# Graph attention with residual and normalisation: late residuals on VectorE, two normalisations on GpSimd, and the last block's leading column searched in halves

## The chip, the cores and the metric

The kernel runs on one core of a Trainium2 chip. The metric is the time of one execution on the device in microseconds; lower is better. The times before are the median of three runs; the profile is of one further execution with the hardware profiler on.

## The reference

```python
def reference(x, adj, W, a):            # x 4096x512, adj 4096x4096, W 512x2048, a 4x1024x1, all float32
    ht  = (x @ W).reshape(N, 4, 512).transpose(1, 0, 2)
    src = einsum('hnd,hd->hn', ht, a[:, :512, 0]); dst = einsum('hnd,hd->hn', ht, a[:, 512:, 0])
    e   = leaky_relu(src[:, :, None] + dst[:, None, :], 0.01) + adj[None]
    g   = einsum('hij,hjd->hid', softmax(e), ht).mean(axis=0)
    x   = x + g
    return (x - mean(x)) / sqrt(var(x) + 1e-5)          # over the 512 columns of each row
```

`adj` is zero or uniform up to 1e9, with a filled diagonal, and is added to the scores ahead of the softmax. Where the largest entry of a row of `adj` leads the second largest by more than the scores can make up for, the softmax is one at that entry's column and zero elsewhere. The row's result is then `layernorm(x[i] + x[column] @ mean over heads of W)`.

## The kernel before, in words

Rows are split into 32 blocks of 128 (`NB`), one row of each block per partition. `leading_rows` treats every row as one with a leading entry and tests that on the side; a second function, `general`, computes the full softmax for blocks in which the test failed, behind a branch that these inputs don't take.

The schedule is written out by hand: engines execute their instructions in the order of the program text. For each step `t` of a loop over the 32 blocks:

- SP's queue issues the load of block `t + 5` of `adj` (2 MB; the last block in four pieces of 128x1024).
- VectorE takes the maxima of segments of 32 columns (`segment_maxima`, L163), then the top 8 of the 128 maxima and their positions (`find_segment`, L170 and L172). GpSimd works out the segment's row in memory (L174) and fetches the segment (`lead`, L176), and works out where it starts (L181).
- Two steps later VectorE takes the fetched segment's top 8 (`inner`, L192; for the blocks from 24 on this is done after the loop) and searches the leading value in it (`find_column`, L198); GpSimd adds the two positions (L200) and gathers the rows of `x` at the leading columns (`y`, L186).
- Three steps later TensorE turns those rows (`turn`, L213), ScalarE copies them out of PSUM (`yt`, L215), and TensorE multiplies them by the mean of `W` over the heads (`products`, L228). The residual is added on TensorE, as a product of the identity with the rows of `x` (`residual`, L221), into the same PSUM tile.
- ScalarE takes mean and variance (`stats`, L250 and L252), GpSimd the factors (`rstd`, L255 to L257), ScalarE normalises (`finish`, L261), and the result goes out from `hold`.

In the code `BEHIND` is 24 and `LATE` is 28. Blocks 24 to 27 have their products put by in SBUF (`put_by`), and the residual is added from there after the loop, on GpSimd for 24 to 26 and on VectorE for 27 (`add_x`, L244). Blocks 28 to 31 are finished after the loop, with VectorE's own statistics (`moments`, L281 and L285) and normalisation (`factor` and `normalise`, L290 and L297). Block 28 and block 29 get their residual on TensorE in the last step of the loop; block 30 on VectorE (L511); block 31 on TensorE, in two halves of 256 columns (`residual_in_halves`, L266).

For block 31 the column isn't searched in the fetched segment but in the whole row, while its segment is fetched for the second largest value only:

```python
    def find_column_in_row(ib):
        col = small.tile([P, 8], U32, name="col")
        nc.vector.max_index(col, top[:, ib, :], adj_t[ib])
        gather_rows(ib, col)
```

The test that all rows have a leading entry needs a bound from the norms of the rows of `x` (`row_norm`, L235). The functions `bound`, `test`, `count` and `report` (L367 to L401) go back and forth between VectorE, TensorE and ScalarE in the midst of the last blocks. The stores of the last blocks are issued by SP in a fixed order: block 28, block 29, blocks 24 and 25, block 30, blocks 26 and 27, block 31.

Of the kernel before, what the change touches and what calls it, by code (L numbers as in the profile page):

```python
# [9 lines left out]
F32 = mybir.dt.float32  # L10
U32 = mybir.dt.uint32
# [9 lines left out]
P = 128  # L21
# [45 lines left out]
def leading_rows(ctx, tc, x, adj, W, a, out, ident, v, n_bad, any_bad):  # L67
# [36 lines left out]
    w_sum = once.tile([P, KB, D], F32, name="w_sum")  # L104
    a_rows = once.tile([2 * H, D], F32, name="a_rows")

    once.tile([P, 32], F32, name="pad_end")
    adj_t = {}

    def pieces(ib):  # L110
# [36 lines left out]

    top = once.tile([P, NB, 8], F32, name="top")
    inner = once.tile([P, NB, 8], F32, name="inner")
    xx = once.tile([P, NB], F32, name="xx")  # L150
    nm = once.tile([P, NB], F32, name="nm")
    sd = once.tile([P, NB], F32, name="sd")
# [4 lines left out]
    def segment_maxima(ib, lo, hi):  # L157

        if lo == 0:
            seg_of[ib] = small.tile([P, S], F32, name="seg")  # L160
        n = max(pieces(ib), 2)
        for k in range(lo * n // PIECES, hi * n // PIECES):
            nc.vector.tensor_reduce(  # L163
                seg_of[ib][:, ts(k, S // n)],
                adj_t[ib][:, ts(k, N // n)].rearrange("p (s e) -> p s e", e=E), axis=AX.X, op=OP.max,
            )

    def find_segment(ib):
        seg = seg_of.pop(ib)
        nc.vector.max(out=top[:, ib, :], in_=seg)  # L170
        at = small.tile([P, 8], U32, name="at")
        nc.vector.max_index(at, top[:, ib, :], seg)  # L172
        row = small.tile([P, 1], U32, name="row")
        nc.gpsimd.tensor_tensor(row, at[:, 0:1], first[:, ib : ib + 1], op=OP.add)  # L174
        lead = lead_pool.tile([P, E], F32, name="lead")
        nc.gpsimd.indirect_dma_start(  # L176
            out=lead, out_offset=None, in_=adj_segs,
            in_offset=bass.IndirectOffsetOnAxis(ap=row[:, :1], axis=0),
        )
        start = at_of[ib] = small.tile([P, 1], U32, name="start")  # L180
        nc.gpsimd.tensor_tensor(start, at[:, 0:1], width, op=OP.mult)  # L181
        lead_of[ib] = lead

    def gather_rows(ib, col):
        y = y_t[ib] = y_pool.tile([P, D], F32, name="y")
        nc.gpsimd.indirect_dma_start(  # L186
            out=y, out_offset=None, in_=x,
            in_offset=bass.IndirectOffsetOnAxis(ap=col[:, :1], axis=0),
        )
# [10 lines left out]
        nc.gpsimd.tensor_tensor(col, at_of.pop(ib), within[:, 0:1], op=OP.add)  # L200
        gather_rows(ib, col)

    def find_column_in_row(ib):

        col = small.tile([P, 8], U32, name="col")
        nc.vector.max_index(col, top[:, ib, :], adj_t[ib])
        gather_rows(ib, col)

    def turn(ib):
        y = y_t.pop(ib)  # L210
        tp = psum.tile([P, KB, P], F32, name="tp", bufs=2)
        for kb in range(KB):
            nc.tensor.transpose(tp[:, kb, :], y[:, ts(kb, P)], ident)  # L213
        yt = yt_of[ib] = rows.tile([P, KB, P], F32, name="yt")
        nc.scalar.copy(yt, tp)  # L215

    def residual(ib):
        start = ib not in o_ps
        if start:
            o_ps[ib] = psum.tile([P, D], F32, name="o")  # L220
        nc.tensor.matmul(o_ps[ib], ident, hold[:, ib, :], start=start, stop=False)  # L221

    def products(ib, lo=0, hi=KB):
        start = ib not in o_ps
        if start:
            o_ps[ib] = psum.tile([P, D], F32, name="o")
        for kb in range(lo, hi):
            nc.tensor.matmul(  # L228
                o_ps[ib], yt_of[ib][:, kb, :], w_sum[:, kb, :],
                start=(start and kb == 0), stop=(kb == KB - 1),  # L230
            )
# [11 lines left out]
    def add_x(engine, ib):  # L243
        engine.tensor_add(hold[:, ib, :], hold[:, ib, :], o_ps["by"][:, ib - BEHIND, :])  # L244
        o_ps[ib] = hold[:, ib, :]
# [8 lines left out]
    def rstd(i):  # L254
        nc.gpsimd.tensor_scalar(sd[:, i], sd[:, i], 1.0 / D, EPS, op0=OP.mult, op1=OP.add)  # L255
        nc.gpsimd.tensor_tensor(sd[:, i], sd[:, i], power[:, : i.stop - i.start], op=OP.pow)  # L256
        nc.gpsimd.tensor_mul(nm[:, i], nm[:, i], sd[:, i])  # L257

    def finish(ib):
        i = slice(ib, ib + 1)  # L260
        nc.scalar.activation(hold[:, ib, :], o_ps.pop(ib), AF.Identity, bias=nm[:, i], scale=sd[:, i])  # L261

    def residual_in_halves(ib):
        o_ps[ib] = [psum.tile([P, D // 2], F32, name="o") for _ in range(2)]
        for k, o in enumerate(o_ps[ib]):
            nc.tensor.matmul(o, ident, hold[:, ib, ts(k, D // 2)], start=True, stop=False)  # L266
# [10 lines left out]
    def moments(ib):  # L277

        if ib < NB - 1:
            st = small.tile([P, nc.vector.BN_STATS_DIM], F32, name="st", bufs=2)  # L280
            nc.vector.bn_stats(st, o_ps[ib])  # L281
        else:
            st = halves_st
        mv = mean_var[ib] = small.tile([P, nc.vector.BN_AGGR_DIM], F32, name="mv", bufs=3)
        nc.vector.bn_aggr(mv, st)  # L285
        r = rt[ib] = sd[:, ib : ib + 1]
        nc.scalar.activation(r, mv[:, 1:2], AF.Sqrt, bias=eps)

    def factor(ib, shift=False):
        nc.vector.reciprocal(rt[ib], rt[ib])  # L290
        if shift:
            nc.vector.scalar_tensor_tensor(
                nm[:, ib : ib + 1], mean_var[ib][:, 0:1], -1.0, rt[ib], op0=OP.mult, op1=OP.mult
            )

    def normalise(ib, o, columns=slice(0, D)):
        nc.vector.tensor_scalar(  # L297
            hold[:, ib, columns], o, mean_var[ib][:, 0:1], rt[ib], op0=OP.subtract, op1=OP.mult
        )
# [108 lines left out]
    for t in range(NB):  # L408
        if t == NB // 2:
            tc.mark_branch_hint_location("general", engines=HINTED)  # L410
        if t in x_at:
            load_x(*x_at[t])
        if t + AHEAD == NB - 1:
            load_x(LATE, Q)
        load_adj(t + AHEAD)
        middle = 1 if t == NB - 1 else 2
        segment_maxima(t, 0, middle)
        if t >= COLUMN:
            find_column(t - COLUMN)
        segment_maxima(t, middle, PIECES)  # L420
        pair = FINISH <= t < BEHIND + FINISH and t % 2 == 0
        if pair:
            rstd(slice(t - FINISH, t - FINISH + 2))
        if t == NB - 1:
            for ib in (BEHIND, BEHIND + 2):
                load_x(ib, 2)
        find_segment(t)
        if t < 2:
            mean_of_heads(t)
        elif t == 2:  # L430
            mean_of_heads(2)
            mean_of_heads(3)
        if t == 0:
            turn_a()
        turned = [(*vectors[0], turn_w(*vectors.pop(0))) for _ in range(vectors_at.get(t, 0))]
        if t == 16:
            head_norms()
        ib = t - PROJECT
        if t == NB - 1:
            for late in range(LATE, NB):  # L440
                row_norm(late)
            residual(LATE)
            residual(LATE + 1)
        if ib >= 0:
            turn(ib)
            if ib > BEHIND:
                products(ib - 1, KB - 1, KB)
            if ib < BEHIND:
                residual(ib)
        for some in turned:  # L450
            head_vector(*some)
        if ib >= 0:
            products(ib, 0, KB if ib < BEHIND else KB - 1)
        if t >= BEHIND + STATS:
            put_by(t - STATS)
        elif t >= STATS:
            stats(t - STATS)
            row_norm(t - STATS)
        if pair:
            finish(t - FINISH)  # L460
            finish(t - FINISH + 1)
# [6 lines left out]
        store(nc.sync, ib, 2)  # L468
    find_column(NB - 2)
    add_x(nc.gpsimd, BEHIND)  # L470
    add_x(nc.gpsimd, BEHIND + 1)
    find_column_in_row(NB - 1)
    add_x(nc.gpsimd, BEHIND + 2)
    products(LATE, KB - 1, KB)
    residual_in_halves(NB - 1)
    turn(NB - 3)
    products(NB - 3, 0, KB - 1)
    moments(LATE)
    for ib in range(BEHIND, NB):
        find_inner(ib)  # L480
    bound(0)
    products(NB - 3, KB - 1, KB)
    stats(BEHIND)
    factor(LATE)
    normalise(LATE, o_ps.pop(LATE))
    bound(1)
    turn(NB - 2)
    bound(2)
    add_x(nc.vector, LATE - 1)
    stats(BEHIND + 1)  # L490
    moments(LATE - 1)
    products(NB - 2, 0, 2)
# [4 lines left out]
    stats(BEHIND + 2)  # L497
    rstd(slice(BEHIND, BEHIND + 2))
    rstd(slice(BEHIND + 2, BEHIND + 3))
    moments(NB - 3)  # L500
    report(pg)
    turn(NB - 1)
# [5 lines left out]
    products(NB - 2, KB - 1, KB)  # L508
    products_of_half(NB - 1, 0)
    products_of_half(NB - 1, 1)  # L510
    nc.vector.tensor_add(hold[:, NB - 2, :], o_ps[NB - 2], hold[:, NB - 2, :])  # L511
    o_ps[NB - 2] = hold[:, NB - 2, :]
    moments(NB - 2)
    stats_of_half(NB - 1, 0)
    factor(NB - 2)
    normalise(NB - 2, o_ps.pop(NB - 2))
    finish(BEHIND + 2)
    finish(BEHIND + 3)
    stats_of_half(NB - 1, 1)
    moments(NB - 1)  # L520
    factor(NB - 1, shift=True)
# [157 lines left out]
```

## Time and profile before

| What | Value |
|---|---|
| median of 3 runs | 236.11 us (235.84 to 236.12) |
| profiled execution | 236.21 us, of which span 234.6 us |
| TensorE (PE) busy | 195.2 us, 83% |
| VectorE (DVE) busy | 188.4 us, 80% |
| ScalarE (ACT) busy | 111.6 us, 48% |
| GpSimd (POOL) busy | 101.2 us, 43% |
| DMA | 97.21 MB, 414 GB/s over the span |
| granted TensorE clock, mean | 0.975 |

Busy shares are means over the whole span. The DMA engines are busy nine tenths or more from the second slice of 40 to the last but two, and the page's chain of work that ended last is DMA for 45% of the span. The timeline lists instructions with start and duration in microseconds from the span's start; a bracket gives the engine's idle time just before and what ended it. L-numbers are lines of the kernel before.

### The profile page before, as it was taken

Reading aid. Unit: us, or ns where it says so; the run is one execution under the profiler, and the core shown is the slowest. Engines: PE = TensorE matmul, PEld = TensorE weight load, DVE = VectorE, ACT = ScalarE, POOL = GpSimd, SP = SyncE. Lnnn points to the kernel's source line nnn. Section 1 sums busy time; section 2 is a strip of 40 time slices with the busy share of each in tenths; the row PEclk is TensorE's granted clock in tenths of the full one; section 3 lists DMA queues with packets and bytes.
Section 4 is the critical chain, followed back from the end, with each engine's and each line's share of the span. In section 5 each row is a group of like instructions: output and inputs, shape, how many; then the busy total and the mean of one; then the engine's idle time right before and its main releaser. Section 6 shows DMA issues by size and latency. Waiting matters only on the chain.

```text
span 234.6 us, 2498 instructions
## 1 busy us (share of the span) xinstructions
PE 195.2 (83%) x683; PEld 101.4 (43%) x683; DVE 188.4 (80%) x302; ACT 111.6 (48%) x267; POOL 101.2 (43%) x215
## 2 busy tenths in 40 slices
PE   0188929999999999999979879797998968698990
PEld 0034514756565655555534333242443423244460
DVE  1736875589869995999589989998799999989672
ACT  2012011255474747474758354646464645166582
POOL 1012232414527462646353645464365464549130
PEclk9999977999999999999999999999799999999998
DMA  6999999999999999999999999999999999999985
GB/s 226 439 428 426 443 425 430 415 440 412 440 420 426 424 437 434 425 424 428 427 432 433 425 433 422 432 418 429 425 432 418 422 425 427 411 425 419 417 355 210
DMA packets 13697, 97.21 MB, mean 414 GB/s; under 512 B 2152, under 2 KB 2664, under 8 KB 7792
## 3 DMA queue, kind: packets, MB, share of 16 engines
q1 hardware_dynamic: 10080, 88.08, 88.9%
q0 software_dynamic: 3584, 8.92, 9.6%
q8 instruction: 6, 0.10, 0.2%
q14 instruction: 11, 0.09, 0.1%
q10 hardware_dynamic: 16, 0.02, 0.0%
HBM read 88.62 MB, written 8.39 MB: 414 GB/s over the span
## 4 chain that ended last, share of the span: by engine, by line
DMA 45%; POOL 17%; issue 15%; PE 10%; DVE 9%; ACT 1%; POOLq 0%; SPq 0%; DVEq 0%
DMA adj_t<-in_adj_dram 42%; DVE seg L163 8%; PE o L228 7%; POOL lead L176 6%; POOL y L186 5%; DMA y<-in_x_dram,col 3%; POOL sd L256 2%; PE o L270 2%; POOL start L181 1%; POOL row L174 1%; POOL col L200 1%; PE tp L213 1%; PE o L221 1%; ACT yt L215 1%; POOL sd L255 1%
## 5 line engine op out<-in xcount | busy, mean ns | idle before, releaser
L163 DVE TENSOR_REDUCE seg<-adj_t 128x64 f32<-128x2048 f32 (+1 forms) x68 | 146.0, 2149 | 32.7 <-DMA adj_t<-in_adj_dram 32.3
L228 PE MATMUL o<-w_sum,yt 128*128 128x512 f32 x248 | 115.1, 605 | 1.7 <-ACT yt L215 1.7
L228 PEld LDWEIGHTS o<-w_sum,yt 128*128 128x128 f32 x248 | 44.5, 191 | 54.8 <-issue 42.3
L215 ACT COPY yt<-tp 128x512 f32<-128x512 f32 x32 | 18.8, 588 | 44.3 <-PE tp L213 44.3
L176 POOL DMA_INDIRECT lead<-in_adj_dram,row x32 | 32.3, 1010 | 15.5 <-POOL row L174 15.0
L186 POOL DMA_INDIRECT y<-in_x_dram,col x32 | 30.9, 965 | 15.4 <-POOL col L200 15.2
L318 PE MATMUL o<-hold,ident 128*128 128x512 f32 x32 | 18.9, 745 | 17.5 <-DMA hold<-in_L_gnn_W_dram 17.5
L213 PE MATMUL tp<-ident,y 128*128 128x128 f32 x128 | 20.0, 280 | 12.6 <-DMA y<-in_x_dram,col 12.6
L221 PE MATMUL o<-hold,ident 128*128 128x512 f32 x52 | 27.3, 611 | 0.0
L213 PEld LDWEIGHTS tp<-ident,y 128*128 128x128 f32 x128 | 14.9, 143 | 25.4 <-issue 25.0
L174 POOL TENSOR_TENSOR row<-at,first 128x1 uint32<-128x1 uint32 x32 | 6.1, 190 | 42.0 <-DVE at L172 42.0
L336 ACT COPY wt<-tp 128x512 f32<-128x512 f32 x16 | 9.2, 587 | 31.4 <-PE tp L334 31.4
L200 POOL TENSOR_TENSOR col<-start,within 128x1 uint32<-128x1 uint32 x31 | 5.9, 190 | 40.1 <-DVE within L198 40.1
L235 ACT ACTIVATE sq<-hold 128x512 f32<-128x512 f32 x32 | 19.8, 619 | 0.0
L342 PEld LDWEIGHTS pv<-at_d,wt 128*128 128x128 f32 x128 | 16.3, 191 | 6.8 <-ACT wt L336 4.0
L318 PEld LDWEIGHTS o<-hold,ident 128*128 128x128 f32 x32 | 7.4, 243 | 26.7 <-POOL row L174 11.0
L319 ACT ACTIVATE w_sum<-o 128x512 f32<-128x512 f32 x4 | 2.4, 598 | 33.9 <-PE o L318 33.9
L261 ACT ACTIVATE hold<-o,nm,sd 128x512 f32<-128x512 f32 x24 | 17.2, 771 | 0.0
L252 ACT ACTIVATE sq<-o,nm 128x512 f32<-128x512 f32 x24 | 16.5, 688 | 0.8
L342 PE MATMUL pv<-at_d,wt 128*128 128x2 f32 x128 | 15.3, 244 | 0.6 <-ACT wt L336 0.6
L250 ACT ACTIVATE sq<-o 128x512 f32<-128x512 f32 x24 | 14.6, 609 | 0.0
L334 PEld LDWEIGHTS tp<-ident,hold 128*128 128x128 f32 x64 | 7.9, 142 | 6.9 <-issue 6.9
(85 smaller groups left out, 139.8 us busy)
## 6 DMA issues: line engine op xcount, KB each, us to landing
adj_t<-in_adj_dram SPq DMA_DIRECT2D x27, 2048.0 KB, 31.3
hold<-in_x_dram SPq DMA_DIRECT2D x7, 1024.0 KB, 33.2
adj_t<-in_adj_dram SPq DMA_DIRECT2D x6, 1024.0 KB, 25.7
out_dram<-hold SPq DMA_DIRECT2D x10, 512.0 KB, 15.2
adj_t<-in_adj_dram SPq DMA_DIRECT2D x8, 512.0 KB
hold<-in_L_gnn_W_dram SPq DMA_DIRECT2D x4, 1024.0 KB
out_dram<-hold SPq DMA_DIRECT2D x2, 1024.0 KB
hold<-in_x_dram SPq DMA_DIRECT2D x2, 512.0 KB, 14.1
```

The lines of the kernel that those rows point to most:

```text
L163: nc.vector.tensor_reduce(seg_of[ib][:, ts(k, S // n)], adj_t[ib][:, ts(k, N // n)].rearrange("p (s e) -> p s e", e=E), axis=AX.X, op=OP.max,)
L176: nc.gpsimd.indirect_dma_start(out=lead, out_offset=None, in_=adj_segs, in_offset=bass.IndirectOffsetOnAxis(ap=row[:, :1], axis=0),)
L186: nc.gpsimd.indirect_dma_start(out=y, out_offset=None, in_=x, in_offset=bass.IndirectOffsetOnAxis(ap=col[:, :1], axis=0),)
L213: nc.tensor.transpose(tp[:, kb, :], y[:, ts(kb, P)], ident)
L215: nc.scalar.copy(yt, tp)
L221: nc.tensor.matmul(o_ps[ib], ident, hold[:, ib, :], start=start, stop=False)
L228: nc.tensor.matmul(o_ps[ib], yt_of[ib][:, kb, :], w_sum[:, kb, :], start=(start and kb == 0), stop=(kb == KB - 1),)
L235: nc.scalar.activation(sq, hold[:, ib, :], AF.Square, accum_out=xx[:, ib : ib + 1])
L252: nc.scalar.activation(sq, o, AF.Square, bias=nm[:, i], accum_out=sd[:, i])
L261: nc.scalar.activation(hold[:, ib, :], o_ps.pop(ib), AF.Identity, bias=nm[:, i], scale=sd[:, i])
L318: nc.tensor.matmul(o, ident, hold[:, w_at + kb * H + h, :], start=(h == 0), stop=(h == H - 1))
L342: nc.tensor.matmul(pv[:, kb, h : 2 * H : H], wt[:, k, :], at_d[:, k, h : 2 * H : H], start=(k == 0), stop=(k == KB - 1),)
```

## The change

Four things are moved or replaced, all of them from the last step of the loop on:

- The residuals of blocks 28 and 29 leave TensorE. VectorE adds them from PSUM (`add_residual`) ahead of the statistics; block 28 is then normalised by ScalarE (`finish`) rather than by VectorE. `residual_in_halves` of block 31 comes after the turn of block 29 rather than before it.
- The residual of block 27 is added by GpSimd rather than by VectorE.
- Blocks 26 and 27 are normalised by GpSimd (`finish_on_chip`) rather than by ScalarE.
- Block 31 has no segments. VectorE takes the top 8 of each quarter of the row as it lands, then the top 8 of each half from those, and searches each half for its own top 8. One comparison of the two halves' largest values chooses the position. The search of the first half is in the loop's last step, ahead of `find_column` of block 30; the second comes after it. The row's top 8 is taken from the two halves' afterwards, and the segment isn't fetched. `inner` of this block is set to the lowest number at the start.

On GpSimd the gather of block 31 now comes after the first of the `add_x` and not after the second.

```diff
-    once.tile([P, 32], F32, name="pad_end")
+    once.tile([P, 80], F32, name="pad_end")
...
     inner = once.tile([P, NB, 8], F32, name="inner")
+    nc.gpsimd.memset(inner[:, NB - 1, :], LOWEST)
...
-    def find_column_in_row(ib):
-
-        col = small.tile([P, 8], U32, name="col")
-        nc.vector.max_index(col, top[:, ib, :], adj_t[ib])
+    quarter8 = once.tile([P, PIECES, 8], F32, name="quarter8")
+    half8 = once.tile([P, 2, 8], F32, name="half8")
+    half_at = once.tile([P, 2, 8], U32, name="half_at")
+    second = once.tile([P, 1], F32, name="second")
+    base = once.tile([P, 1], F32, name="base")
+
+    def quarter_maxima(ib, lo, hi):
+
+        for k in range(lo, hi):
+            nc.vector.max(out=quarter8[:, k, :], in_=adj_t[ib][:, ts(k, N // PIECES)])
+
+    def half_maxima(ib):
+
+        for k in range(2):
+            nc.vector.max(out=half8[:, k, :], in_=quarter8[:, ts(k, 2), :].rearrange("p k e -> p (k e)"))
+
+    def find_in_half(ib, k):
+        nc.vector.max_index(half_at[:, k, :], half8[:, k, :], adj_t[ib][:, ts(k, N // 2)])
+
+    def choose_half(ib):
+
+        nc.vector.tensor_tensor(second, half8[:, 1, 0:1], half8[:, 0, 0:1], op=OP.is_gt)
+        nc.vector.scalar_tensor_tensor(
+            base, half_at[:, 0, 0:1], float(N // 2), second, op0=OP.subtract, op1=OP.mult
+        )
+        nc.vector.tensor_sub(base, half_at[:, 0, 0:1], base)
+
+    def gather_rows_by_halves(ib):
+        col = small.tile([P, 1], U32, name="col")
+        nc.vector.tensor_scalar(col, half_at[:, 1, 0:1], second, base, op0=OP.mult, op1=OP.add)
         gather_rows(ib, col)
+        nc.vector.max(out=top[:, ib, :], in_=half8.rearrange("p k e -> p (k e)"))
...
+    def finish_on_chip(ib):
+        i, h = slice(ib, ib + 1), hold[:, ib, :]
+        o_ps.pop(ib)
+        nc.gpsimd.tensor_scalar(h, h, sd[:, i], nm[:, i], op0=OP.mult, op1=OP.add)
+
+    def add_residual(ib):
+        nc.vector.tensor_add(hold[:, ib, :], o_ps[ib], hold[:, ib, :])
+        o_ps[ib] = hold[:, ib, :]
...
-        middle = 1 if t == NB - 1 else 2
-        segment_maxima(t, 0, middle)
+        last = t == NB - 1
+        if last:
+            quarter_maxima(t, 0, 1)
+        else:
+            segment_maxima(t, 0, 2)
         if t >= COLUMN:
             find_column(t - COLUMN)
-        segment_maxima(t, middle, PIECES)
+        if last:
+            quarter_maxima(t, 1, PIECES)
+        else:
+            segment_maxima(t, 2, PIECES)
...
-        if t == NB - 1:
+        if last:
             for ib in (BEHIND, BEHIND + 2):
                 load_x(ib, 2)
-        find_segment(t)
+            half_maxima(t)
+            find_in_half(t, 0)
+        else:
+            find_segment(t)
...
             for late in range(LATE, NB):
                 row_norm(late)
-            residual(LATE)
-            residual(LATE + 1)
...
     find_column(NB - 2)
     add_x(nc.gpsimd, BEHIND)
+    choose_half(NB - 1)
+    find_in_half(NB - 1, 1)
+    gather_rows_by_halves(NB - 1)
     add_x(nc.gpsimd, BEHIND + 1)
-    find_column_in_row(NB - 1)
     add_x(nc.gpsimd, BEHIND + 2)
+    add_x(nc.gpsimd, BEHIND + 3)
     products(LATE, KB - 1, KB)
+    turn(NB - 3)
     residual_in_halves(NB - 1)
-    turn(NB - 3)
     products(NB - 3, 0, KB - 1)
+    add_residual(LATE)
     moments(LATE)
-    for ib in range(BEHIND, NB):
+    for ib in range(BEHIND, NB - 1):
         find_inner(ib)
     bound(0)
     products(NB - 3, KB - 1, KB)
     stats(BEHIND)
-    factor(LATE)
-    normalise(LATE, o_ps.pop(LATE))
+    factor(LATE, shift=True)
+    finish(LATE)
     bound(1)
     turn(NB - 2)
     bound(2)
-    add_x(nc.vector, LATE - 1)
...
+    add_residual(NB - 3)
     moments(NB - 3)
...
-    nc.vector.tensor_add(hold[:, NB - 2, :], o_ps[NB - 2], hold[:, NB - 2, :])
-    o_ps[NB - 2] = hold[:, NB - 2, :]
+    add_residual(NB - 2)
     moments(NB - 2)
...
-    finish(BEHIND + 2)
-    finish(BEHIND + 3)
+    finish_on_chip(BEHIND + 2)
+    finish_on_chip(BEHIND + 3)
```

## The prediction

> **What bounds the kernel now.** I read the page for shares, then the chain of waits, then the timeline of the last 35 us engine by engine. The page's chain gives 45% to DMA, nearly all of it matrix blocks being streamed, and the DMA row is full until the last slices. The change touches nothing before the last of the 32 block steps, so the streaming stays as it is and only the tail counts. The chain of waits through the tail (start us, duration us, what):
>
> ```profile
> 196.17 7.27 DMA y<-in_x_dram,col
> 203.44 0.14 issue
> 203.58 0.63 PE tp L213 x4
> 204.21 3.57 PE o L228 x8
> 207.78 1.72 PE o L221 x4
> 209.49 0.44 PE tp L213 x4
> 209.93 4.38 PE o L228 x10
> 214.31 0.86 PE o L266 x4
> ...
> 220.09 0.45 PE tp L213 x4
> ...
> 225.69 3.55 PE o L270 x16
> ```
>
> From 203.58 to 229.24 TensorE hardly stops: blocks 27, 28, 29, 30, 31 are turned (L213) and multiplied (L228, L270) in a row, then 2 us of small steps and the last store end the span. The 1.72 us of L221 are the residuals of blocks 28 and 29. The next lines, from the timeline of VectorE and GpSimd (start, duration, engine, line), show what feeds those turns:
>
> ```profile
> 204.97 0.09 DVE L198 MATCH_VALUE_LOAD within<-top,lead 128x8 f32 x1 [0.18 <-DMA lead<-in_adj_dram,row]
> 208.87 0.30 DVE L170 MAX8 top<-seg 128x8 f32<-128x128 f32 x1
> 210.08 0.09 DVE L198 MATCH_VALUE_LOAD within<-top,lead 128x8 f32 x1 [0.45 <-DMA lead<-in_adj_dram,row]
> 210.42 4.42 DVE L206 FIND_INDEX8 col<-top,adj_t 128x8 uint32<-128x4096 f32 x1
> 212.00 0.97 POOL L186 DMA_INDIRECT y<-in_x_dram,col  x1 [0.27 <-POOL col L200]
> 215.65 0.96 POOL L186 DMA_INDIRECT y<-in_x_dram,col  x1 [0.16 <-PE tp L213]
> 219.27 0.28 DVE L371 TENSOR_REDUCE xg<-px 1x1 f32<-1x128 f32 x1 [1.81 <-PE px L369]
> ```
>
> The reader is to see three things: the column of block 30 is found at 210.34, its rows are asked for at 212.00; the column of block 31 takes a 4.42 us search; and VectorE has only 1.81 us of idle time in front of L371. So TensorE's queue bounds the tail, but with little room behind it.
>
> **How soon gathered rows can be turned** decides the rest. Where TensorE waited for them, gather start to turn was 185.51 to 192.49, 190.84 to 197.60 and 196.17 to 203.58: 6.98, 6.76 and 7.41 us. In these three the turn began 0.7, 0.4 and 0.5 us after the last packet of the software queue (DMA view in 0.1 us windows). For blocks 28, 29 and 30 the last packets were at 207.1, 212.6 and 218.1; with 0.5 added they could be turned at 207.6, 213.1 and 218.6, which is 6.1, 7.05 and 6.6 us after their starts. Mean of the six 6.8, from 6.1 to 7.4.
>
> **What the Trainium skill says.** "GPSIMD Engine Reference", Elementwise — side-by-side cycle accounting, puts a two-input add on GpSimd at about 2.6 cycles per element at 1.2 GHz, 1.11 us for 512 columns before dispatch; the trace agrees with 1.27 to 1.29 us (L244). The same section gives a good one-input loop 769 ns for 512 elements; no large one is in the trace. "Vector Engine (DVE) Microarchitecture Reference", The match/index hardware and the swap-based sort pattern, says that a top 8 streams values through eight sorting cells and that positions need a separate search; so one value per cycle should hold for both. "DMA: Bandwidth & Descriptors", SWDGE vs HWDGE vs iDMA, says that each DMA engine round-robins between the software queue and the hardware one; the trace shows it, with 49.7% and 49.8% of the engines for a gather's packets at 216.5 to 217.5 beside the stores.
>
> **Part 1, the search of block 31.** Four L163 reduces of 128x1024 (1.21 us each) become four top 8s. L192 takes 0.184 us for 32 columns, L170 0.295 for 128: 1.16 ns per column at most, 1.04 if it goes like FIND_INDEX8 (0.285 for 128, 4.42 for 4096). So 1.23 to 1.33 each; I take 1.24, +0.1 in all (up to +0.5). The reduces ended at 208.84; now 208.95. Then two top 8s of 16 (0.3 with the wait), a value load and a search of 2048 columns (0.285+1920x1.04 ns = 2.29, +0.09). Only then comes the search for block 30, which is queued behind it on VectorE: 208.95+0.3+0.1+2.38+0.25 = 212.0 instead of 210.34, **1.65 us later**. Three ops on 128x1 at the 0.16 pitch of L377/L378 (0.48), the second half (2.38) and the column (0.15) give 215.0 against 214.84 before: no gain there, though 0.37 us of segment search and 4.5 of row search went.
>
> On GpSimd, three instructions of block 31's segment go (row 0.19, gather 0.97 after 0.51 of issue, start 0.20). Before, they held block 30's column until 211.54. Now it runs at 212.08, and its gather 0.72 later, as at 200.78 to 201.50 where GpSimd also had waited for VectorE: **212.8 instead of 212.00**. Block 31's gather follows one add instead of two, once its column is there: some 215.4 instead of 215.65.
>
> **Part 2, residuals off TensorE.** The two L221 matmuls go, 1.72 us on the path. Turn 28 moves to 207.78 (its rows are there at 207.6), and 0.44+4.38 later, at 212.6, TensorE reaches turn 29, which now waits for rows until 213.1. The halves' residuals (L266, 0.86) are behind turn 29 now and cover ScalarE's copy, where TensorE had idled 0.66 (215.62 to 216.28). Three products take it to 217.05. The row maximum xm is the next thing that TensorE waits for. On VectorE: column at 215.0, top 8 0.2, block 28's add 0.69, statistics 0.72, aggregate 0.18, seven instead of eight top 8s 0.7, xm 0.17: 217.6 (216.46 before). So TensorE stands 0.5 us, then px and one product: it is ready for turn 30 at **218.6**, 1.4 us ahead of the 219.93 of before.
>
> **Part 3, where that gain stops.** Block 30's rows, asked for at 212.8, can be turned at 212.8+6.8 = **219.6**. TensorE waits 1 us for them; before they had been there 1.3 us early. Turn 30 gains 219.93-219.6 = 0.3 us. This is the sum that I forecast; what follows must keep within it:
> - ScalarE: root of block 28 at 216.8, two statistics (1.75 from the root's start), normalisation of block 28 (0.80, moved here from VectorE's 0.81), root of xg to 219.5: before turn 30's copy at 220.3. No cost.
> - GpSimd: add 24 to 215.1, gather 31 from 215.4, three adds of 1.27 to 220.25. So block 27's statistics start at 220.3 against 220.18; VectorE's add (0.67, L244) is gone and it waits for GpSimd instead. Test (1.38 after the aggregate's start), add 29 (0.69), statistics, aggregate: 223.9 to 224.1; ScalarE's root of 29 and the copy of turn 31 end by 224.9 to 225.1, where TensorE needs it at 225.2 (225.51 before, less 0.3). Cover of 0.1 to 0.3 us; beyond 0.6 us of gain this chain ends last.
> - Rows of block 31: 215.4+6.8 = 222.2, needed at 224.1.
> - Blocks 26 and 27 normalised on GpSimd from 225.3: by the skill's one-input price 0.77 each, by the nearest row (a two-input add) 1.27: done at 226.8 to 227.9 against 229.10 on ScalarE. The last store waits for block 31 (L310, to 231.25), so nothing is gained. It costs only if the two end after 231.2, that is at over 2.9 us each.
> - Block 28's store leaves SP's queue 1.8 us later (its normalisation ended at 217.5); stores then took 15.2 us to land in a full queue, so the DMA engines lack no work. The memset of 8 columns is on an idle GpSimd at the start; the padding adds no instruction. Both nothing; no cover could go.
>
> The end from turn 30 on is as before: -0.3 us. The profiled execution took 236.21 (span 234.6 and 1.6 around it), so 235.9 with a profile; the median is 236.11, so **235.8**.
>
> **Rivals.**
> 1. *Block 30's rows come later still* (slower). Break-even is a gather of 7.1 us, which one of six exceeded and one nearly met. With top 8s at 1.33 us (+0.35) and a gather of 7.4, turn 30 is at 220.55, +0.6: 236.7. It decides from a turn 30 after 219.93, and passes the noise after 220.4. For it: the search is put ahead of block 30 on an engine with no slack. Against: five of six gathers were under 7.1.
> 2. *They come early.* At 6.1 to 6.6 us turn 30 is at 218.9 to 219.4; then VectorE, the root of 29 and the copy of turn 31 bound the end: -0.5 to -0.7, 235.5. For: block 28's gather was 6.1, block 30's own 6.6.
> 3. *The whole TensorE saving arrives*: 1.72+0.66 = 2.4, 233.7. Against: VectorE's xm at 217.6 alone stops it a microsecond short.
> 4. *The normalisations on GpSimd end last*, above 2.9 us each: nothing in the trace or the skill points there; at 3.3 each +0.8, 236.9.
>
> **How the numbers follow.** A difference of 0.2% is 0.47 us, about what these runs can tell from none. Forecast 0.50 (235.6 to 236.5), rival 1 beyond the noise 0.21, rival 2 beyond the noise 0.25, rival 3 0.02, rival 4 0.02. Faster 0.27, same 0.50, slower 0.23. The range leaves out rival 3 and the ends of rivals 1 and 2: 235.3 to 236.9.
>
> **What would show it.** In the profile after: no L221 pair in the last step; turn 29 with an idle time that ended with the gathered rows; block 30's gather at 212.8 and its turn waiting about 1 us for DMA; L371's wait for TensorE gone or small; block 27's statistics waiting for GpSimd at 220.3; two GpSimd TENSOR_SCALARs of 128x512 at 0.8 to 1.3 us. It is wrong if turn 30 waits for nothing, if a top 8 of 1024 takes much over 1.33 us, or if the end moves by over 0.7 us either way.

## The result and the profile after

The changed kernel takes **237.15 us** (median of 20 runs, 236.51 to 239.87), the kernel before beside it on the same chip 236.05 (20 runs, 235.84 to 237.10). The ratio over all runs is **1.0058, 95% interval 1.0041 to 1.0075** (the two medians alone give 1.0047): slower by about 0.6%, and above the forecast range. The 20 times lie in two groups, 11 at 236.5 to 237.2 (median 236.62) and 9 at 238.0 to 239.9. The profiled execution, 236.79 us with a span of 235.2, belongs to the lower one; against the profile before (236.21, span 234.6) it shows where 0.6 us went. That is the difference of the lower group from the kernel before; the rest of the 1.1 us between the medians is the upper group, which gets its own experiments. "Turn 29" below is TensorE's turning of the gathered rows of block 29, and "the copy of turn 29" is ScalarE's copy of them out of PSUM, which the products of that block wait for.

The chain of waits of the kernel after, from 217 us on (start us, duration us, what):

```profile
217.00 0.09 DVE xm L404
217.09 0.08 DVE sd L327
217.17 0.02 issue
217.19 3.05 DVE nm L329
220.24 0.03 issue
220.27 0.81 ACT hold L289
221.08 0.09 ACT xg L409
221.17 0.47 ACT yt L243
221.65 0.04 issue
221.69 1.98 PE o L256 x4
...
226.18 3.55 PE o L307 x16
```

From 209.19 to 217.17 the chain is on VectorE (the searches of blocks 31 and 30, their columns, the add and moments of block 28, and small steps). Then it stands for 3.05 us in one instruction on 128x1, passes through ScalarE, and reaches TensorE only at 221.69. The last products start at 226.18, where they started at 225.69 before. Here is that instruction with its neighbours, from the timelines of VectorE, GpSimd and ScalarE (start, duration, engine, line; in brackets the idle time ahead and what ended it):

```profile
217.19 3.04 DVE L329 SCALAR_TENSOR_TENSOR nm<-mv,sd 128x1 f32<-128x1 f32 x1
216.50 3.70 POOL L272 TENSOR_TENSOR hold<-hold,adj_t 128x512 f32<-128x512 f32 x3
220.27 0.81 ACT L289 ACTIVATE hold<-hold,nm,sd 128x512 f32<-128x512 f32 x1 [2.11 <-DVE nm L329]
221.08 0.56 ACT L243 COPY yt<-tp 128x512 f32<-128x512 f32 x1
```

`factor(LATE, shift=True)`, which the ScalarE normalisation of block 28 needs, computes minus the mean times the reciprocal root of the variance: the shift, which ScalarE adds when it normalises. It reads two tensors in SBUF, starts 0.69 us after GpSimd began its three adds, and ends at 220.23; the adds end at 220.20. By source line:

```profile
L329 DVE SCALAR_TENSOR_TENSOR nm<-mv,sd x3: 159/160/3039, 217.2 to 231.0; 128x1 f32<-128x1 f32 x3
```

The shortest, median and longest of this line's three instructions are 159, 160 and 3039 ns: the shifts of blocks 27 and 31 take a nineteenth of the time. ScalarE has its normalisation (L289) queued ahead of the root of xg (a step of `bound`) and of the copy of turn 30. The copy starts at 221.08 instead of 220.57, and the 0.5 us stay to the end: the last half is normalised at 231.18 instead of 230.69. ScalarE before, and the last half after:

```profile
220.57 0.59 ACT L215 COPY yt<-tp 128x512 f32<-128x512 f32 x1 [0.78 <-PE tp L213]
230.69 0.56 ACT L310 ACTIVATE hold<-o,nm,sd 128x256 f32<-128x256 f32 x1 [0.42 <-DVE nm L292]
231.18 0.56 ACT L347 ACTIVATE hold<-o,nm,sd 128x256 f32<-128x256 f32 x1 [0.43 <-DVE nm L329]
```

The other part is on TensorE (its timeline: start, duration; turns 28, 29 and 30 before, then after):

```profile
209.33 0.60 PE L213 MATMUL tp<-ident,y 128*128 128x128 f32 x4
215.01 0.60 PE L213 MATMUL tp<-ident,y 128*128 128x128 f32 x4
219.93 0.60 PE L213 MATMUL tp<-ident,y 128*128 128x128 f32 x4
207.80 0.63 PE L241 MATMUL tp<-ident,y 128*128 128x128 f32 x4 [1.07 <-DMA y<-in_x_dram,col]
214.89 0.63 PE L241 MATMUL tp<-ident,y 128*128 128x128 f32 x4 [2.09 <-DMA y<-in_x_dram,col]
219.84 0.60 PE L241 MATMUL tp<-ident,y 128*128 128x128 f32 x4
```

The residuals of blocks 28 and 29 are gone. Turn 28 begins 1.53 us earlier than the 209.33 of before. Turn 29 then waits 2.09 us for rows and begins at 214.89, against 215.01. Turn 30 begins at 219.84, against 219.93, and waits for no rows. Nine hundredths of a microsecond are left of the 2.4 (the residuals' 1.72 and the idle 0.66) that the change took off TensorE's queue.

### The profile page after: what moved, and what is told of

Same layout as the page of the kernel before. It is cut to its first block, busy times and chain, and to the rows that moved or that the text cites. A ratio compares the mean times of both kernels' runs of the same rounds, so it can differ in the third digit from the quotient of the medians.

```text
span 235.2 us, 2495 instructions
## 1 busy us (share of the span) xinstructions
PE 192.4 (82%) x679; PEld 99.2 (42%) x679; DVE 190.9 (81%) x308; ACT 110.9 (47%) x266; POOL 102.5 (44%) x216
## 4 chain that ended last, share of the span: by engine, by line
DMA 74%; DVE 18%; PE 4%; issue 1%; ACT 1%; SPq 0%; DVEq 0%
DMA adj_t<-in_adj_dram 74%; DVE seg L164 11%; PE o L256 2%; PE o L307 2%; DVE half_at L221 1%; DVE nm L329 1%; DVE within L199 1%; DVE quarter L213 1%; DVE inner L193 1%; DVE at L173 0%; DVE top L171 0%; ACT hold L289 0%; DVE st L318 0%; DVE hold L297 0%; ACT hold L347 0%
## 5 line engine op out<-in xcount | busy, mean ns | idle before, releaser
L164 DVE TENSOR_REDUCE seg<-adj_t 128x64 f32<-128x2048 f32 (+1 forms) x64 | 141.3, 2209 | 32.7 <-DMA adj_t<-in_adj_dram 32.3
L177 POOL DMA_INDIRECT lead<-in_adj_dram,row x31 | 31.3, 1009 | 15.5 <-POOL row L175 15.5
L355 PE MATMUL o<-hold,ident 128*128 128x512 f32 x32 | 18.6, 732 | 15.3 <-DMA hold<-in_L_gnn_W_dram 15.3
L241 PEld LDWEIGHTS tp<-ident,y 128*128 128x128 f32 x128 | 14.3, 141 | 30.7 <-issue 29.8
L249 PE MATMUL o<-hold,ident 128*128 128x512 f32 x48 | 24.7, 596 | 0.5 <-DMA hold<-in_x_dram 0.5
L289 ACT ACTIVATE hold<-o,nm,sd 128x512 f32<-128x512 f32 x24 | 17.2, 769 | 0.0
```

The lines of the kernel that those rows point to most:

```text
L164: nc.vector.tensor_reduce(seg_of[ib][:, ts(k, S // n)], adj_t[ib][:, ts(k, N // n)].rearrange("p (s e) -> p s e", e=E), axis=AX.X, op=OP.max,)
L177: nc.gpsimd.indirect_dma_start(out=lead, out_offset=None, in_=adj_segs, in_offset=bass.IndirectOffsetOnAxis(ap=row[:, :1], axis=0),)
L355: nc.tensor.matmul(o, ident, hold[:, w_at + kb * H + h, :], start=(h == 0), stop=(h == H - 1))
```

## The experiments

The expectations call the runs by label: e1_one_read is experiment 1, e4_row_search experiment 5, and e5_again experiment 8. "nm" is the shift, and an "upper group" is one of times some 1.5 us above the others.

**Theory:** the change by itself neither gains nor loses, since rows cap what TensorE saves; the loss is one VectorE instruction held by GpSimd's adds. The Trainium skill, "SBUF — State Buffer", Who interferes with whom, says that a VectorE instruction with two SBUF inputs contends with a GpSimd instruction that reads SBUF, and that one with at most one SBUF input, outside the two-port modes, does not. **Rivals:** the search of halves, the normalisations on GpSimd, or late rows make the loss.

**1. The shift with one SBUF tensor.** Edit on the kernel after:

```diff
-        if shift:
+        if shift and ib == LATE:
+            nc.vector.tensor_scalar(
+                nm[:, ib : ib + 1], mean_var[ib][:, 0:1], rt[ib], -1.0, op0=OP.mult, op1=OP.mult
+            )
+        elif shift:
```

> Changed kernel with one edit: the factor nm of block 28 is a TENSOR_SCALAR (one SBUF tensor, one pointer scalar) instead of a SCALAR_TENSOR_TENSOR (two SBUF tensors). In the changed kernel that instruction lasted 3.04 us instead of 0.16, from 217.19 to 220.23, and GpSimd's three adds ended at 220.20. Theory (a VectorE instruction that reads two SBUF tensors waits until GpSimd's run of adds is over): it lasts 0.16 us, block 28 is normalised on ScalarE at 218.2 instead of 220.27, turn 30's copy starts at 220.5 instead of 221.08, profiled time 236.2 instead of 236.8. Rival a (small instructions whose inputs are in SBUF wait too): it lasts 3 us as before, 236.8. Rival b (the 3 us are not on the path): 0.16 us, and 236.8 all the same. The upper half of the changed kernel's runs, near 238.2, stays if its cause is the landing of the last quarter, and goes if it is this wait.

Measured: 235.97 us (22 runs), ratio 0.9999 (0.9984 to 1.0014). From VectorE's timeline of this kernel:

```profile
217.44 0.21 DVE L329 TENSOR_SCALAR nm<-mv,sd 128x1 f32<-128x1 f32 x1
220.50 0.69 DVE L318 BATCH_NORM_STATS2 st<-hold 128x6 f32<-128x512 f32 x1 [0.95 <-POOL hold L272]
```

Beside the same adds it takes 0.21 us. The copy of turn 30 is back at 220.57. The second line is the wait that the forecast had named (block 27's statistics wait for GpSimd), and it costs nothing. The loss is gone, within the interval, although turn 29 came as late as in the kernel after (214.98 against 214.89): so late rows don't make it. Two of the 22 runs are at 237.7 to 237.8, so the upper group is smaller than the 9 of 20, but not gone.

**2. The shift on ScalarE.** Two small ACTIVATEs replace it.

```diff
+            nc.scalar.activation(nm[:, ib : ib + 1], neg28, AF.Identity, scale=rt[ib])
...
+    nc.scalar.activation(neg28, mean_var[LATE][:, 0:1], AF.Identity, scale=-1.0)
```

> Changed kernel with nm of block 28 worked out on ScalarE (the negated mean, then times the factor) and no VectorE instruction in its place. Theory: VectorE has nothing to wait for beside the adds, L408 follows TensorE's px at about 219.2 and block 28 is normalised at about 218.6 on ScalarE; turn 30's copy starts at 220.5 to 220.6, profiled time 236.2 to 236.3. Rival b: 236.8. Rival c (another VectorE instruction takes the wait, the reciprocal or the row maximum): that one lasts 3 us and the time stays 236.8.

Measured: 236.27 (22 runs), ratio 1.0016 (1.0004 to 1.0028). Most of the loss is gone here too. In its profile (235.56) turn 29 happened to begin at 214.27 and turn 30 at 219.22, both 0.71 us earlier than in experiment 1; the spread of the row gathers is as large as what is being measured, so the 0.16% is not read further.

**3. The same form, with one input in PSUM.** A TENSOR_SCALAR is another form of instruction, so experiment 1 left open whether the form or the place of the operand matters.

```diff
+            again = psum.tile([P, 1], F32, name="pv", bufs=1)
+            nc.vector.reciprocal(again, rt[ib])
...
+            nc.vector.scalar_tensor_tensor(nm[:, ib : ib + 1], mean_var[ib][:, 0:1], -1.0, again, op0=OP.mult, op1=OP.mult)
```

> The changed kernel, with the shift of block 28 in the same form of instruction at the same place (SCALAR_TENSOR_TENSOR of mean and reciprocal root), but the reciprocal that it reads as its second tensor is written to PSUM by an additional reciprocal of 0.15 us ahead of it; the three adds on GpSimd stay. Theory (two tensors read from SBUF wait for GpSimd's run of adds, one does not): 0.16 to 0.25 us instead of 3.04, ending at 217.8 and not with the adds at 220.2, ScalarE's normalisation of block 28 before 219, time as without the loss: 235.9 to 236.4. Rival (the form of instruction, the write to SBUF, or the order on VectorE makes it wait, not where the second tensor lies): it ends with the adds at 220.2 to 220.4 and the time stays at 236.6 to 237.2.

Measured: 236.03 (14 runs), ratio 1.0011 (0.9992 to 1.0030). VectorE and GpSimd:

```profile
217.12 0.16 DVE L329 RECIPROCAL pv<-sd 128x1 f32<-128x1 f32 x1
217.40 0.14 DVE L332 SCALAR_TENSOR_TENSOR nm<-mv,pv 128x1 f32<-128x1 f32 x1
216.61 3.71 POOL L272 TENSOR_TENSOR hold<-hold,adj_t 128x512 f32<-128x512 f32 x3
```

0.14 us at 217.40, while the adds run. The rival of the form has fallen: what waits is the second SBUF input.

**4. The search alone** (the kernel before with the top 8s of quarters and the two half searches, and nothing else of the change).

> Kernel before with only the search of block 31 changed (quarters, halves, no segment fetched); residuals of 28 and 29 stay on TensorE, blocks 26 and 27 stay on ScalarE, block 27's residual on VectorE. Theory (the cost is the wait of nm beside three adds, and nm of block 28 doesn't exist here): within 0.3 us of before, 235.9 to 236.4. Rival d (the search makes block 30's rows late or puts the last quarter's landing on the path): 236.5 or more, with a second group of runs near 238.

Measured: 235.92 (14 runs), ratio 1.0001 (0.9984 to 1.0019). Block 30's gather starts at 212.40 and block 31's at 215.42, and turn 29 does not wait. The search costs nothing.

**5. The change with the old search.**

> Changed kernel with only the search put back (segments, segment of block 31 fetched, whole row searched); the residuals stay on VectorE and GpSimd, blocks 26 and 27 on GpSimd. GpSimd's order is add, add, gather of block 31, add, add. Theory: nm of block 28 again waits for the adds, which now end at about 219.2 instead of 220.2, so it lasts about 1.5 us; turn 30 starts at 219 to 219.5, profiled time 235.6 to 236.2. Rival d (the search is what costs): no runs near 238, all within 235.3 to 236.3; if the second group near 238 is there as well, the search is not its cause.

Measured: 236.41 (14 runs), ratio 1.0006 (0.9987 to 1.0024). In the profiled execution (237.86) two adds stand after the last gather instead of three:

```profile
217.71 1.86 DVE L301 SCALAR_TENSOR_TENSOR nm<-mv,sd 128x1 f32<-128x1 f32 x1
217.03 2.51 POOL L244 TENSOR_TENSOR hold<-hold,adj_t 128x512 f32<-128x512 f32 x2
```

The shift ends at 219.57 and the adds at 219.54, so the hold follows the adds in length; it ends 0.66 us earlier than in the kernel after, and no loss can be told from none. The old search has long times too (237.86 and 238.12, 2 of 14), so the new one isn't their only source. This profile is of one of them. In the windows view (stretch, its length, busy us of PE, PEld, DVE, ACT and POOL, granted TensorE clock, DMA share, GB/s):

```profile
213.00:215.00 2.00, 0.14 (x2) 0.17 (x3) 2.00 (x1) 0.00 (x0) 1.98 (x3) 1.00 0.97 406
217.00:219.00 2.00, 2.00 (x4) 0.73 (x3) 1.97 (x9) 1.54 (x5) 1.99 (x3) 0.50 1.03 420
```

TensorE stood idle for 2.00 us ahead of turn 29 (214.86); from 216.0 to 219.4 its clock is granted at 0.50. The six products then take 4.24 us instead of the 2.81 of the kernel after: 1.43 us, about the distance of the two groups.

**6 and 7. Two spare products early** (at block steps 10 and 11, result unused), to shift TensorE's instruction stream: once on experiment 1, once on the kernel after.

```diff
+        if t in (10, 11):
+            fill = psum.tile([P, D], F32, name="tp", bufs=2)
+            nc.tensor.matmul(fill, ident, w_sum[:, 0, :], start=True, stop=True)
```

> e1_one_read with two spare products of 512 columns on TensorE in steps 10 and 11 of the loop, into a PSUM tile that nobody reads, so that TensorE's instruction stream has the length of before's again. In six profiles so far a 16 KB instruction packet of queue q8 took one DMA engine for 0.95 us at 201.1 to 201.2 in the two kernels that keep the L221 residuals and at 211.2 to 211.5 in the four that don't, and the gather under way at that moment landed late: block 27's in the former (turn 27 at 203.6 to 203.9, else 202.5 to 202.8), block 29's in the latter (8.0 to 8.7 us, turn 29 at 214.3 to 215.0). Theory (the packet delays block 29's rows): it falls near 200 to 201 again, block 29's rows can be turned at 213.1 to 213.7, turn 30 at 218.6 to 219.6, time 235.4 to 235.7. Rival (the gather is late for another reason, such as the stores beside it): turn 29 at 214.3 to 215.0 as in e1_one_read, 235.9 to 236.4.

> The changed kernel with only those two spare products. Theory: turn 29 comes earlier as above, but the factor of block 28 still waits for GpSimd's third add at 220.2, which the gather of block 31 sets and not TensorE, so the lower group of runs stays at 236.5 to 236.8. The upper group near 238: if it comes from TensorE's idle 2 us ahead of turn 29, after which its clock is granted at half, it goes; if from the idle 0.8 to 1.2 us ahead of L412 and the products of block 30, which wait for ScalarE behind that factor, it stays with some 9 in 20.

Measured: 236.41 (22 runs), ratio 1.0019 (1.0000 to 1.0039) with the shift of experiment 1; 237.87 (8 runs), ratio 1.0068 (1.0044 to 1.0093) without. No gain in either, and the packet fell at 206.2 and 206.7 us, not at 200 to 201. Long times stayed in both: 6 of 22 above 237.55, and 4 of 8 above 238. The late gather moved from turn 29 to turn 28 (table below). The profile of experiment 7 (237.52) waited 2.56 us ahead of turn 28 and then had the clock at 0.50 from 210.7 to 214.1.

**8 and 9. The kernel after, unchanged, profiled twice more.**

> The changed kernel unchanged, profiled again, to see an execution of its upper group (9 of 20 runs). Theory (clock): if the time is near 238.3, the granted TensorE clock is 0.5 for some 3.4 us after turn 29 and its matmuls there take 1.4 us longer, as in the profile of e4_row_search (237.86: six products of block 29 in 4.24 us instead of 2.81). Rival (a late landing): clock 1.0 throughout the tail, and a turn that waits over 2.5 us for rows or a last quarter that comes after 208.5. If the time is near 236.7, nothing follows.

> The changed kernel unchanged, profiled once more, with the same expectations as in the run named e5_again: near 238.3 a granted clock of 0.5 after turn 29 by the theory, or clock 1.0 and a late landing by the rival.

Measured: 236.95 and 237.13. The shift took 1.91 us (218.41 to 220.32, adds to 220.30) and 3.04 us (from 217.64; adds to 220.66). With experiment 7 (1.81 us from 219.09; adds to 220.87), experiment 5 and experiment 11 (3.04 from 217.16; adds to 220.18), all six profiles of the two-input form end within 0.03 us of GpSimd's last add, whether they start in the first add or the second. So the wait lasts over the whole uninterrupted run of adds and not just the one under way. Neither profile fell into the upper group, so no execution of the unchanged kernel after in that group has been profiled. Experiment 8 did have the clock at 0.50, from 210.4 to 213.9, and the ten products of block 28 took 6.18 us instead of 4.54; yet at 236.95 it lies in the lower group. Turn 29 then waited for nothing; turn 30 came 0.78 us later than in the first profile after, but the copy of turn 30, which had waited for the shift there, only 0.17 later. A stretch at half the clock alone doesn't make a long time: it depends on which products it falls on.

**10 and 11. Two spare products ahead of turn 28 and two ahead of turn 29,** on experiment 1 and on the kernel after, to keep TensorE from standing idle.

```diff
+        for k in range(2):
+            nc.tensor.matmul(spare, ident, w_sum[:, k, :], start=True, stop=True)
```

> The changed kernel with the shift of block 28 from one SBUF tensor, and two spare products (identity by summed weights, result unused) ahead of turn 28 and two ahead of turn 29, where TensorE waits 1.1 to 2.5 us and 1.9 to 2.1 us for gathered rows. Theory (a wait of 2 us and more lets the clock fall to half for about 3.4 us in part of the executions, and this makes the upper group of times): the waits seen at the turns fall by 1.2 to 1.4 us to under 1.3 us, no run with half a clock between 208 and 222 us, nothing above 237 us where the same kernel without spare products had 2 of 22 and its neighbour 6 of 22, median 235.6 to 236.0. Rival (the upper group has another cause, such as rows that land late): a tenth to a quarter of the runs stay at 237.6 to 238.3. Second rival (the spare products themselves delay the turns): everything 0.3 to 0.7 us later, median above 236.4.

> The changed kernel as it is, with two spare products (result unused) ahead of turn 28 and two ahead of turn 29. Theory (two losses that add: the shift of block 28 held by the adds, 0.5 us, and the clock at half after a wait in part of the executions): the shift still takes 3 us and ends with the adds at 220.2 us; the group of 9 in 20 at 238.0 to 239.9 us is gone and the runs lie at 236.4 to 236.9, median 236.6, ratio 1.002 to 1.003. Rival (the held shift alone makes the upper group too): the median stays at 237.1 and a third or more of the runs stay above 237.9.

Measured: 237.04 (6 runs, none above 237.51), ratio 1.0043 (1.0029 to 1.0057), and 236.84 (6 runs, 236.59 to 237.16), ratio 1.0038 (1.0026 to 1.0051). The kernel after lost its group at 238.0 and above (9 of 20 runs without the spare products, 0 of 6 with them; six runs are few) and kept the rest: its shift still takes 3.04 us. On experiment 1 the second rival came true. A pair takes 1.88 us, not the 1.2 to 1.4 that I had put down, so turn 29 waits for nothing any more and everything is 0.8 us later (TensorE, and the products after turn 30, at 221.21 in experiment 1):

```profile
215.82 0.60 PE L241 MATMUL tp<-ident,y 128*128 128x128 f32 x4
222.02 1.99 PE L261 MATMUL o<-w_sum,yt 128*128 128x512 f32 x4 [0.37 <-ACT yt L243]
```

**12. The normalisations of blocks 26 and 27 back on ScalarE,** on experiment 1.

```diff
-    finish_on_chip(BEHIND + 2)
-    finish_on_chip(BEHIND + 3)
+    finish(BEHIND + 2)
+    finish(BEHIND + 3)
```

> The changed kernel with the shift of block 28 from one SBUF tensor, and the normalisations of blocks 26 and 27 back on ScalarE; the residuals stay on VectorE. Theory (the move of the two normalisations to GpSimd is worth nothing either way): GpSimd has no normalisation at 226 to 228 us, ScalarE has two of 0.81 us there, the end does not move, ratio to the kernel before 0.999 to 1.001, as with them on GpSimd. Rival 1 (GpSimd's two reads of SBUF hold VectorE's last statistics): faster than with them by 0.2 us or more. Rival 2 (ScalarE's last half waits behind the two): slower by 0.2 us or more.

Measured: 236.19 (22 runs), ratio 1.0018 (0.9997 to 1.0039). The interval holds both no difference and 0.2 us, but the profiles of this kernel and of experiment 3 can be laid on each other, as their turns 30 begin at the same 219.58. ScalarE with the two normalisations:

```profile
227.26 1.50 ACT L289 ACTIVATE hold<-hold,nm,sd 128x512 f32<-128x512 f32 x2
230.35 0.56 ACT L351 ACTIVATE hold<-o,nm,sd 128x256 f32<-128x256 f32 x1 [0.42 <-DVE nm L333]
```

and in experiment 3, with them on GpSimd:

```profile
230.34 0.57 ACT L354 ACTIVATE hold<-o,nm,sd 128x256 f32<-128x256 f32 x1 [0.42 <-DVE nm L336]
```

The last half ends at the same time. In these profiles the move is worth nothing either way.

**13. One spare product ahead of each of the two turns,** on experiment 1.

> The changed kernel with the shift of block 28 from one SBUF tensor, and one spare product (0.94 us, result unused) ahead of turn 28 and one ahead of turn 29, where two each delayed turn 29 by 0.8 us and turn 30 by the same. Theory (the wait for rows lets the clock fall in part of the executions, and a product that fits inside the wait costs nothing): the waits at the turns are 0.1 to 1.6 us instead of 1.05 to 2.5, turn 29 stays at 214.3 to 215.0, no run above 237.2 us, median 235.5 to 235.9, ratio 0.998 to 1.000. Rival (one product leaves waits long enough for the clock to fall, or rows land early enough in most executions for it to delay the turn): some runs stay at 237.6 to 238.3, or the lower group moves up to 236.2 and more.

Measured: 236.01 (14 runs, 235.43 to 237.28), ratio 0.9997 (0.9980 to 1.0014). Turn 29 began at 215.05 after a wait of 0.69, so the product (1.02) lies inside the wait. The longest time is 237.28, a little over the 237.2 that I had set, and none is at 237.6 or above. The median, a little above the 235.9 expected, stays where it was: this does not beat the kernel before either, and no version run here does.

Over experiments 1, 2, 3, 6 and 12 (the hold gone, no products ahead of the turns) 16 of 102 runs were above 237.55; with products ahead of the turns (10, 11, 13) none of 26. The kernel before, run beside all of these, was there once in 159 runs (238.07). The mean granted clock of every run is on record, and 3.4 us at half lower it by some 0.007 (an estimate from the stretches seen, over a span of 235 us). In the kernel after it was 0.957 to 0.970 in the 9 long runs, and above 0.970 in 6 of the 11 others; in the five experiments it was above 0.970 in 1 of the 16 long runs and in 53 of the 86 others. That, with the clock of experiment 5, is the case for a half clock after a wait as the cause of the long times. No profile shows it for the kernel after, and why that has so many of them (9 of 20) is not settled.

## Why the prediction was wrong

**The step that failed** is in part 3, the entry on ScalarE: "normalisation of block 28 (0.80, moved here from VectorE's 0.81) ... No cost". A move to ScalarE also brings the shift that ScalarE needs as a bias, and this new VectorE instruction was in no sum. At the duration of its form, 0.16 us, it would have been covered. It took 3.04 because the adds on GpSimd, which the same list puts up to 220.25, stand beside it. ScalarE's normalisation started 2.11 us later than it could have; the copy of turn 30 could have borne some 1.5 of that (it would have started at about 220.48, 0.64 after the turn as before); the rest, less the 0.09 gained by turn 30, is the 0.5 us of the end. Experiment 1 frees this one instruction, and the copy is back at its place. The forecast asked of each moved operation when its engine is free and when its inputs are ready, and not what shares its path to SBUF.

**The terms that were mis-sized.** They don't make the loss, but they took the forecast gain of 0.3 us: with the shift freed, turn 30 stood at 219.93 in experiment 1, as before the change, and not at 219.6.
- Turn 29 "waits for rows until 213.1": 214.89. The DMA view of the kernel after from 212.9 to 214.5 (packets, MB, share of 16 engines) has

```profile
q0 software_dynamic: 3, 0.01, 1.3%
```

  77 of the gather's 80 packets had landed by 212.8, which with the 0.5 us of the forecast gives 213.3. The three stragglers began at 213.3, 213.8 and 214.3.
- TensorE "ready for turn 30 at 218.6": 219.84, by those stragglers. xm (the row maximum of `bound`), which was to hold it, was done at 217.09 instead of 217.6.
- "Block 30's rows at 219.6" were to decide: their last packet landed at 218.2, 5.7 us after the gather's start at 212.49, so they could be turned by about 218.7. TensorE was the later one. Rival 1 (these rows later still) has fallen, and rival 2 (they come early) had no effect, since turn 29 had used up the gain first.

**What was right:** the top 8 of 1024 columns at 1.21 to 1.23 us (1.24 forecast) and the half searches at 2.29; block 30's gather at 212.49 (212.8) and block 31's at 215.51 (215.4); turn 28 at 207.80 (207.78); the normalisations on GpSimd, inside the bounds and at no cost. The timeline of GpSimd has

```profile
226.17 1.52 POOL L294 TENSOR_SCALAR hold<-hold,sd,nm 128x512 f32<-128x512 f32 x2
```

0.76 us each, beside the 769 ns of the Trainium skill, "GPSIMD Engine Reference", Elementwise — side-by-side cycle accounting. Rival 4 has fallen with this, and rival 3 by the wait at turn 29. Without the held instruction the number comes near the forecast: experiment 1 measured 235.97, inside the range and within 0.2% of no change. That is in part luck: block 30's rows, which were to decide, came early, and block 29's, which were not, came late. The sign of the loss came from a mechanism that none of the rivals named.

## What to carry to other kernels

When an operation moves to another engine, list every small instruction that prepares its operands, and look at what runs beside each of them: here a VectorE instruction on 128x1 with two SBUF inputs waited 3 us for three long adds on GpSimd, and one input from a pointer or from PSUM freed it. Before a gain on the busiest engine is counted, ask when the next input arrives: the time taken off TensorE became a wait for rows within two blocks. A wait on TensorE can cost more than its length, as the products behind it may run at half the clock (six took 4.24 us instead of 2.81 in experiment 5).

## What the runs showed of the hardware

- **The hold lasts as long as GpSimd's run.** The Trainium skill, "SBUF — State Buffer", Who interferes with whom, says of VectorE's two-port modes that whoever issues first has the pair of SBUF ports that they share with GpSimd for the whole instruction. Six profiles here, of an instruction with two SBUF inputs, show more than one instruction's length: 3.04 us in three, 1.91, 1.86 and 1.81, each up to the end of the last of two or three back-to-back adds, at 1.24 us or so each.
- **A clock of half after about 2 us of idleness.** The Trainium skill, "TensorE: Matmul & The Clock Gate", Part 1, has the clock fall after an idle window of about 3.4 us that runs freely. The stretches at 0.5 are 3.4 us long here (216.0 to 219.4 in experiment 5, 210.7 to 214.1 in experiment 7, 210.4 to 213.9 in experiment 8), which agrees with the window's length. But the idle time ahead of the turn was only 2.00, 2.56 and 2.48 us, so less than a window of idleness was enough; the stretch began 0.8 to 1.2 us after the turn. A wait of 2.09 us in the first profile after, or 2.47 in experiment 6, was followed by a full clock.
- **A packet of an instruction queue takes a DMA engine, and the gather under way then ends late.** In each of these profiles one 16 KB packet of an instruction queue falls into this part. The kernel after, 211.3 to 212:

```profile
q8 instruction: 1, 0.02, 8.4%
```

  8.4% of 16 engines in 0.7 us is one engine for 0.94 us.

| kernel | the packet at | turn that waited longest for rows | its wait |
|---|---|---|---|
| before | 201.2 | 27, at 203.58 | 1.84 |
| experiment 4 | 201.2 | 27, at 203.88 | 2.17 |
| experiment 6 | 206.2 | 28, at 209.41 | 2.47 |
| experiment 7 | 206.7 | 28, at 209.91 | 2.56 |
| experiment 8 (kernel after) | 206.1 | 28, at 209.21 | 2.48 |
| kernel after | 211.4 | 29, at 214.89 | 2.09 |
| experiment 9 (kernel after) | 211.9 | 29, at 215.30 | 1.99 |
| experiment 1 | 211.5 | 29, at 214.98 | 1.93 |

  The longest of the gathers that the forecast had used (7.41 us, block 27 before) is one of these. In the three profiles of the table in which the packet came at 206 to 207, turn 29 waited for nothing. Experiments 2, 3, 5 and 12 have the packet at 211.2 to 211.6, and turn 29 waited longest there, for 1.49 to 2.00 us. The rows come late where the packet falls; that the packet is the cause is argued from the order of times alone, since no run could take it away. What places it is open, for the same kernel had it at 206.1 and at 211.4.
